# A planned fp32 factorization kernel: first loads entered in the planner's model, X sums in wide operations, two zero matmuls instead of three

## The chip, the core and the metric

The kernel runs on one core of a Trainium2 chip. The core has five engines that work beside each other and wait for one another by semaphores: TensorE (PE: matmuls, with weight loads that overlap them), VectorE (DVE), ScalarE (ACT), GpSimd (POOL) and SyncE (SP, which here only issues transfers). Transfers can be issued by SP, ScalarE and GpSimd and run on the core's 16 DMA engines. The metric is the time on the device in microseconds, the median of several runs.

## The reference

`x` is 1024 x 512, `weight` holds 64 matrices of 512 x 512, `lin_w` is 512 x 512, all in fp32.

```python
out_lin = x @ lin_w.T + lin_b
xv = jnp.einsum('bf,efm->bem', x, weight)
zp = jnp.einsum('bf,efm->bem', jnp.square(x), jnp.square(weight))
interaction = 0.5 * jnp.sum(jnp.square(xv) - zp, axis=1)
return out_lin + interaction
```

The sum of `zp` over `e` needs only the weights' squares summed over `e`, so it is one small matmul at the end. The large work is `xv`, 64 products of 1024 x 512 by 512 x 512, whose squares are summed over `e`.

## The kernel before, in words

**The products.** The weights are laid out beforehand in 16 groups `g`, each four quadrants of 1 MB: `w11`, `w12`, `w21`, `w22` (`w22` in two buffers, `w22a` and `w22b`, used by turns). Within a group the product with x is made by a fast scheme with 7 products in place of 8, applied at two levels. At the outer level, seven operands `X1` to `X7` stand for sums of x's quarters, and each meets one of seven right sides: the four quadrants, `T1`, `T2` (sums of quadrants that DMAs accumulate on the way in) and `w12`, `w21` once more with something added to them. At the inner level each pair of an outer operand and a right side is a "tree" of 7 products. The outer operands come in the order `ORDER = (1, 6, 2, 7, 5, 4, 3)`: the first tree is X1 with `w11`, the second X6 with `T2`, the third X2 with `w21`. There are 16 x 7 = 112 trees.

**One tree** (`tree`). GpSimd makes four inner sums of the right side, `t1` to `t4` (each in a ring of two buffers, so `t1_0` and `t1_1`). TensorE makes the products, each of two matmuls of 128 x 512 ("a pair") into a PSUM tile of two banks. PSUM holds four such tiles: `b1`, `b3` and the ring `b2_0`, `b2_1`. Several products add into one tile after its earlier value was copied away: product 5 starts `b3`, ScalarE copies it to a buffer of the ring `p5`, product 3 is added, and the result is copied to one of the ring `p53`; product 1 starts `b1`, ScalarE copies that to `b2_*`, product 6 is added there, VectorE takes `b2 + p53` out (`oa1<-b2,p53`), product 7 is added, and so on. The next tree's product 5 overwrites `b3`, so it waits for the copy to `p53`. The products of neighbouring trees are interleaved by `PLACE`: product p of tree s has the key 7 s + PLACE[p], and TensorE's order is the order of the keys.

**The squares.** The results of the outer scheme are squared on ScalarE and reduced on VectorE into `acc`. The weights' squares are made by `w_squares`: ScalarE squares half a quadrant into a ring of two buffers `wsq`, VectorE reduces it over `e` into `w2_sum`. For `w22a` of the first group these are the pairs `wsq_0<-w22a` and `wsq_1<-w22a`.

**The beginning.** `xT` comes in eight transfers on SP's queue (into `oa0` to `oa3`) and `lin_wT` in four on ScalarE's (into `ob0`, `ob1`). Meanwhile TensorE runs three matmuls on zeros (lines 323 to 328). Then `lin`, x times `lin_wT`: four k-steps of four pairs into all four PSUM tiles, the last pair put behind the first tree's product 5. VectorE adds the bias and takes the tiles out to `ob2`, `ob3`, `c_0`, `c_1`, and SP writes each of these to DRAM (`lind`). Beside `lin`, the X operands are made: outer sums of 1024 elements a partition (`X7`, `X5`, `X6`, `X3` on VectorE; `X1`, `X2`, `X4` copied by ScalarE), then for each operand four inner sums of 256 elements (lines 392 to 402), all on VectorE.

**The planner.** No engine's order is written out by hand except TensorE's. `Plan.add` records each step with its cost on an engine, what it reads and writes by name, and, for transfers, `land`, the time from the end of the issue to the landing. `Plan.order` first gives each step a latest time, backwards from TensorE's order, and then runs a model of the engines: whenever an engine is free it takes the ready step with the earliest latest time, and may leave a short idle for an urgent one that is about to be ready. What comes out is each engine's order of instructions; on the chip every engine takes its own in that order and waits where a semaphore says so. SP is one engine of the model, with a cost of 4.8 us for a load of 1 MB and 2.4 for a smaller one. The transfers of x and `lin_wT` are issued outside of the plan, ahead of all; the planner only knows when they are taken to have landed (`landing`, lines 309 to 319). In the model, SP is free from the start.

A step marked `both` (the X sums, `x_sum`) gets dearer in the model when GpSimd is busy as it starts, and GpSimd's step with it.

Lines that matter in what follows: 247 and 248 (the X tiles), 309 to 319 (`landing`), 323 to 329 (zeros), 373 to 402 (`x_sum` and its uses), 414 to 416 (`load`), 418 to 424 (`load_more`, the accumulating load that GpSimd issues), 426 to 435 (`outer_sum`). In the profile, L276 is any elementwise sum, L288 a copy on ScalarE, L290 a square, L297 a reduction, L304 a transfer of the plan on SP's queue, L326 the zeros, L340 `lin`, L422 an accumulating load, L481 a tree's matmul, L627 the last matmuls.

Of the kernel before, what the change touches and what calls it, by code (L numbers as in the profile page):

```python
# [11 lines left out]
F32 = mybir.dt.float32  # L12
# [4 lines left out]
P = 128  # L17
G = 2
ORDER = (1, 6, 2, 7, 5, 4, 3)
# [4 lines left out]
PE, DVE, ACT, POOL, SP = "PE", "DVE", "ACT", "POOL", "SP"  # L24
# [148 lines left out]
def kernel(  # L173
# [44 lines left out]
    Q = B // 4  # L218

    sb = ctx.enter_context(tc.tile_pool(name="sb", bufs=1))  # L220
# [9 lines left out]
    buf = {}  # L230

    def make(name, shape, pool=sb):
        buf[name] = pool.tile(shape, F32, tag=name, name=name)
        return name
# [9 lines left out]
        return take  # L244

    half = [P, 2, N]
    for i in range(1, 8):
        make(f"X{i}", [P, 7, Q])
    for q in ("w11", "w12", "w21", "w22a", "w22b", "T1", "T2"):
        make(q, [P, 2, 2, N])  # L250
    for pos in range(4):
# [14 lines left out]
    plan = Plan()  # L266
# [3 lines left out]
    def two_input(engine, o, a, b, sub, size=1024):  # L270

        costs = {DVE: 0.08 + 1.06 * size / 1024, POOL: 0.14 + 2.19 * size / 1024}

        def emit(e):
            f = engines[e].tensor_sub if sub else engines[e].tensor_add
            f(o, a, b)  # L276

        return {engine: costs[engine]}, emit
# [24 lines left out]
    def dma(o, i, reads, writes, cost=2.4, land=1.5, queue=nc.sync):  # L303
        plan.add({SP: cost}, lambda _: queue.dma_start(o, i), reads, writes, land=land)  # L304
# [4 lines left out]
    def landing(name, at):  # L309
        plan.add({SP: 0.0}, None, (), (name,), land=at)  # L310

    for k in range(NK):
        q, r = divmod(k, KH)
        x0, x1, l = f"oa{q}", f"oa{2 + q}", f"ob{q}"
        nc.sync.dma_start(buf[x0][:, r, :], x_src[:, k, ts(0, H)])
        nc.scalar.dma_start(buf[l][:, r, :], lw_src[:, k, :])  # L316
        nc.sync.dma_start(buf[x1][:, r, :], x_src[:, k, ts(1, H)])
        for name in (x0, l, x1):
            landing((name, r), 4.0 + 2.5 * k)
    nc.gpsimd.dma_start(bias, lin_b.partition_broadcast(P))  # L320


    zero = buf["t1_0"]
    nc.vector.memset(zero, 0.0)
    for j in range(3):
        nc.tensor.matmul(  # L326
            buf[("b1", "b3")[j // 2]][:, j % 2, :], zero[:, 0:P], zero, start=True, stop=True
        )
    plan.add({PE: 4.0}, None, (), ("b1", "b3"), key=-2000)

    lin_banks = ["b3", "b1", "b2_0", "b2_1"]
    for k in range(NK):
        q, r = divmod(k, KH)
# [16 lines left out]
    for g, bank in enumerate(lin_banks):  # L350
        o = ("ob2", "ob3", "c_0", "c_1")[g]
        for j in range(G):
            costs, emit = two_input(DVE, buf[o][:, j, :], buf[bank][:, j, :], bias, False, 512)
# [3 lines left out]
    def block4(i):  # L357
        return buf[f"X{i}"][:, 0:4, :].rearrange("p (k q) b -> p k (q b)", k=2)
# [3 lines left out]
    def a_parts(*names):  # L362
        return tuple((a_buf[n], r) for n in names if n in a_buf for r in range(KH)) + tuple(
            n for n in names if n not in a_buf
        )

    def a_ap(n):
        return buf[a_buf[n]] if n in a_buf else block4(int(n[1]))
# [1 line left out]
    for i, n in ((1, "A11"), (2, "A12"), (4, "A22")):  # L370
        act(block4(i), a_ap(n), None, a_parts(n), (f"X{i}",))

    def x_sum(i, o, a, b, kind, reads, size):

        if kind != "-a - b":
            costs, emit = two_input(DVE, o, a, b, kind == "a - b", size)
        else:
            costs = two_input(DVE, o, a, b, True, size)[0]

            def emit(_):  # L380
                nc.vector.scalar_tensor_tensor(o, a, -1.0, b, ALU.mult, ALU.subtract)

        plan.add(costs, emit, reads, (f"X{i}",), both=True)

    for i, a, b, kind in (
        (5, "A22", "A21", "a - b"),
        (6, "X5", "A11", "-a - b"),
        (7, "A11", "A21", "a - b"),
        (3, "X6", "A12", "-a - b"),
    ):  # L390
        x_sum(i, block4(i), a_ap(a), a_ap(b), kind, a_parts(a, b), 1024)
    for i in ORDER:
        x = buf[f"X{i}"]
        a11, a21, a12, a22 = (x[:, s, :] for s in range(4))
        s1, s2, s4 = (x[:, s, :] for s in range(4, 7))
        for o, a, b, kind in (
            (s1, a21, a22, "a + b"),
            (s2, s1, a11, "a - b"),
            (s4, a12, s2, "a - b"),
            (a21, a11, a21, "a - b"),  # L400
        ):
            x_sum(i, o, a, b, kind, (f"X{i}",), 256)
    for n in a_buf.values():
        plan.add({SP: 0.0}, None, (), (n,) + tuple((n, r) for r in range(KH)))
    for n in ("ob0", "ob1", "ob2", "ob3", "c_0", "c_1"):
# [5 lines left out]
    def w(g, q):  # L411
        return q + "ab"[g % 2] if q == "w22" else q

    def load(g, q):
        n = w(g, QUAD[q])
        dma(buf[n], weight[g, q], (), (n,), 4.8)

    def load_more(n, src, reads=()):

        plan.add(  # L420
            {POOL: 1.0},
            lambda _: nc.gpsimd.dma_start(buf[n], src, accum_op=ALU.add),  # L422
            (n,) + reads, (n,), land=8.0,
        )

    def outer_sum(g, which):
        if which < 3:
            n = f"T{which}"
            dma(buf[n], weight[g, 0], (), (n,), 4.8)
            for q in (1, 3)[:which]:  # L430
                load_more(n, weight[g, q])
        elif which == 3:
            load_more("w12", weight[g, 3])
        else:
            load_more("w21", buf["T2"], ("T2",))
# [117 lines left out]
    for g in range(NG):  # L553
        acc_name[g] = acc_ring()
        load(g, 0)
        outer_sum(g, 2)
        for q in (1, 2, 3):
            load(g, q)
        outer_sum(g, 1)
        w_squares(g, "w12")  # L560
        for idx, i in enumerate(ORDER):
            if i == 1:
                w_squares(g, "w11")
            if i == 2:
                w_squares(g, "w21")
            if i == 7:
                outer_sum(g, 3)
            if i == 4:
                outer_sum(g, 4)
            if i == 5:  # L570
                w_squares(g, "w22")
            tree(7 * g + idx, g, i)
        if g + 1 < NG:
            names = tuple((acc_name[g], *k) for k in acc_parts)
            dma(acc_dram[:, :, ts(g, MG)], buf[acc_name[g]], names, names + (("accd", g),))
# [13 lines left out]
    for g in range(NB // G):  # L589
        n, a = lin_all[g], acc_all[g]  # L590
# [3 lines left out]
    for n in xe.values():  # L594
        plan.add(
            {DVE: 1.24},
            lambda _, x=buf[n]: nc.vector.scalar_tensor_tensor(
                x, x, -0.5, x, ALU.mult, ALU.mult
            ),
# [13 lines left out]
    for g in range(NB // G):  # L613
        rows = {0: (2, 3), 1: (4, 5)}[g // 2]
        reads = tuple((last, i, 2 * (g % 2) + c) for i in rows for c in range(2))
# [5 lines left out]
    for g, bank in enumerate(("b3", "b1", "b2_0", "b2_1")):  # L621
        o = acc_all[g]
        h = g // 2
        for j in range(G):
            def emit(_, bank=bank, g=g, h=h, j=j):
                for k in range(NK):
# [9 lines left out]
                     key=last_key - 0.5 if (g, j) == (0, 0) else last_key + 1 + 2 * g + j)  # L636
            costs, emit = two_input(
                DVE, buf[o][:, j, :], buf[bank][:, j, :], buf[lin_all[g]][:, j, :], False, 512
            )
# [37 lines left out]
```

## Time and profile before

| what | us |
|---|---|
| median of 3 runs | 1421.0 |
| lowest and highest | 1420.74, 1421.23 |
| the profiled execution | 1420.72 |
| its span, from the first to the last instruction | 1418.9 |

| engine | busy, us | share of the span |
|---|---|---|
| TensorE, matmuls | 1408.6 | 99% |
| VectorE | 1082.0 | 76% |
| GpSimd | 1014.1 | 71% |
| ScalarE | 681.8 | 48% |

The mean granted clock of TensorE is 0.999 of full speed. From about 2 to 58 us the DMA engines are busy throughout, mostly at 200 to 430 GB/s; over the span they move 142 GB/s.

Matmuls are pipelined in the records: one record of 593 ns begins every 0.43 us. So the start times tell more than the durations do. A line of the timeline gives the start in us from the beginning of the span, the duration, the engine, the line of the code, the operation with its output and input tiles (buffer numbers left out, so `X` is any of X1 to X7), the shape, how many instructions were merged into the line, and, in brackets, the idle time of the engine before it and what ended that.

### The profile page before, as it was taken

To read this page: it belongs to the slowest core of one execution; us is meant where nothing else is said; L and a number is where in the kernel's file an instruction comes from. 1 tells how busy PE (TensorE), PEld (TensorE's weight loads), DVE (VectorE), ACT (ScalarE), POOL (GpSimd) and SP (SyncE) were. 2 spreads that over 40 slices of the span, in tenths; PEclk is the share of its full clock that TensorE was granted. 3 is DMA by queue.
4 is the path that set the end of the run, shared out by engine and by line. 5 is a ranking of instruction groups with operands and counts; after the bars stand their busy time and mean duration, and the time that the engine had idled before them with its cause. 6 is when DMAs were issued, how large, how long until landed. Compare 5 with 4: busy or idle time off the path is not lost.

```text
span 1418.9 us, 10383 instructions
## 1 busy us (share of the span) xinstructions
PE 1408.6 (99%) x3270; PEld 621.9 (44%) x3270; DVE 1082.0 (76%) x957; ACT 681.8 (48%) x692; POOL 1014.1 (71%) x693
## 2 busy tenths in 40 slices
PE   9999999999999999999999999999999999999998
PEld 4444444444444444444444444444444444444443
DVE  4779596876958678596877959687795867869685
ACT  2346363554635446373544636355463644537331
POOL 3587786867769686786958678586777868678660
PEclk9999999999999999999999999999999999999999
DMA  9666372655737275472746637265573727546331
GB/s 327 184 162 167 95 179 74 189 123 148 176 88 162 86 182 148 118 178 73 182 108 168 162 100 182 74 182 122 148 181 90 162 79 191 139 123 144 102 106 60
DMA packets 47286, 200.96 MB, mean 142 GB/s; under 512 B 19008, under 2 KB 20032, under 8 KB 24704
## 3 DMA queue, kind: packets, MB, share of 16 engines
q0 software_dynamic: 11600, 84.15, 31.4%
q1 hardware_dynamic: 35056, 115.09, 22.7%
q10 hardware_dynamic: 576, 1.05, 0.2%
q8 instruction: 27, 0.44, 0.1%
q14 instruction: 27, 0.22, 0.0%
HBM read 177.34 MB, written 6.16 MB: 129 GB/s over the span
## 4 chain that ended last, share of the span: by engine, by line
PE 95%; DMA 2%; DVE 2%; POOL 1%; issue 0%; ACT 0%; ACTq 0%; DVEq 0%; SPq 0%
PE b L481 93%; PE b L627 2%; DMA w<-weight 1%; DVE X L276 1%; DMA ob<-lin_wT 1%; POOL ob L276 0%; POOL c L276 0%; DVE w_sum L297 0%; DVE c L276 0%; DVE ob L276 0%; POOL oa L276 0%; ACT oa L290 0%; ACTq L316 0%; POOL t L276 0%; DVE p L276 0%
## 5 line engine op out<-in xcount | busy, mean ns | idle before, releaser
L481 PE MATMUL b<-t,X 128*128 128x512 f32 x1792 | 808.2, 593 | 4.0 <-DVE oa L276 2.6
L481 PEld LDWEIGHTS b<-t,X 128*128 128x128 f32 x1792 | 340.4, 190 | 434.8 <-issue 429.0
L481 PE MATMUL b<-w,X 128*128 128x512 f32 x768 | 358.1, 592 | 0.0
L276 POOL TENSOR_TENSOR t<-w 128x512 f32<-128x512 f32 x128 | 171.2, 1337 | 147.6 <-PE b L481 91.8
L288 ACT COPY p<-b 128x1024 f32<-128x1024 f32 x160 | 161.1, 1007 | 170.6 <-PE b L481 170.6
L481 PEld LDWEIGHTS b<-w,X 128*128 128x128 f32 x768 | 145.9, 190 | 183.7 <-issue 183.4
L276 POOL TENSOR_TENSOR t<-w,t 128x512 f32<-128x512 f32 x128 | 167.7, 1310 | 57.7 <-PE b L481 57.7
L290 ACT ACTIVATE oa<-oa 128x1024 f32<-128x1024 f32 x128 | 133.7, 1057 | 148.0 <-DVE oa L276 146.1
L297 DVE TENSOR_REDUCE acc<-oa 128x16 f32<-128x1024 f32 x128 | 153.7, 1212 | 39.2 <-ACT oa L290 39.2
L481 PE MATMUL b<-T,X 128*128 128x512 f32 x384 | 180.5, 592 | 0.0
L288 ACT COPY b<-b 128x1024 f32<-128x1024 f32 x112 | 111.8, 999 | 141.0 <-PE b L481 140.5
L297 DVE TENSOR_REDUCE w_sum<-wsq 128x16 f32<-128x1024 f32 x128 | 152.2, 1209 | 9.2 <-ACT wsq L290 9.2
L290 ACT ACTIVATE c<-c 128x1024 f32<-128x1024 f32 x64 | 67.6, 1057 | 160.2 <-DVE c L276 93.7
L276 DVE TENSOR_TENSOR oa<-b,p 128x1024 f32<-128x1024 f32 x96 | 116.9, 1218 | 34.5 <-PE b L481 34.5
L276 POOL TENSOR_TENSOR t<-T 128x512 f32<-128x512 f32 x64 | 85.3, 1333 | 65.7 <-issue 35.4
L481 PEld LDWEIGHTS b<-T,X 128*128 128x128 f32 x384 | 73.1, 190 | 92.4 <-issue 84.9
L276 DVE TENSOR_TENSOR p<-b,p 128x1024 f32<-128x1024 f32 x80 | 97.7, 1221 | 20.8 <-PE b L481 19.1
L276 DVE TENSOR_TENSOR ob<-b,p 128x1024 f32<-128x1024 f32 x48 | 58.6, 1221 | 70.2 <-PE b L481 70.2
L290 ACT ACTIVATE wsq<-w 128x1024 f32<-128x1024 f32 x96 | 98.2, 1057 | 15.1 <-DMA w<-weight 13.3
L276 POOL TENSOR_TENSOR t<-T,t 128x512 f32<-128x512 f32 x64 | 86.4, 1350 | 18.1 <-PE b L481 18.1
L276 DVE TENSOR_TENSOR p<-b,oa 128x1024 f32<-128x1024 f32 x32 | 39.2, 1224 | 65.6 <-PE b L481 65.6
L276 DVE TENSOR_TENSOR oa<-b,oa 128x1024 f32<-128x1024 f32 x64 | 78.3, 1223 | 9.8 <-PE b L481 9.7
(55 smaller groups left out, 1338.7 us busy)
## 6 DMA issues: line engine op xcount, KB each, us to landing
w<-weight SPq DMA_DIRECT2D x48, 1024.0 KB, 4.9
T<-weight POOLq DMA_DIRECT2D x48, 1024.0 KB, 8.2
T<-weight SPq DMA_DIRECT2D x32, 1024.0 KB, 4.8
w<-weight POOLq DMA_DIRECT2D x16, 1024.0 KB, 8.2
w<-T POOLq DMA_DIRECT2D x16, 1024.0 KB, 6.9
w22a<-weight SPq DMA_DIRECT2D x8, 1024.0 KB, 11.1
w22b<-weight SPq DMA_DIRECT2D x8, 1024.0 KB, 11.3
oa<-xT SPq DMA_DIRECT2D x8, 256.0 KB, 6.4
```

Source lines behind the costliest of these rows:

```text
L276: f(o, a, b)
L288: nc.scalar.copy(o, i)
L290: nc.scalar.activation(o, i, func)
L297: lambda _: nc.vector.tensor_reduce(o, i.rearrange("p a (m e) -> p a m e", e=E), axis=AX.X, op=ALU.add),
L481: nc.tensor.matmul(buf[b][:, j, :], buf[f"X{i}"][:, SLOT[p], ts(j, P)], op, start=first, stop=True, skip_group_check=True,)
L627: nc.tensor.matmul(buf[bank][:, j, :], buf[xe[h, k // KH]][:, k % KH, ts((g * G + j) % (NB // 2), P)], w2_sum[:, k, :], start=(k == 0), st ...
```

## The change

- The seven X tiles become slices of one tile `x_all`.
- The inner sums of the first operand in ORDER, X1, stay four operations of 256 elements a partition. Those of X2 to X7 become four operations over all six operands, 6 x 256 elements each; in the plan each reads and writes all six names.
- The zero matmuls go to `b1` only, two instead of three. Their cost in the plan stays 4.0.
- The taken landing times of the first loads are 4.3 + 2.6 k in place of 4.0 + 2.5 k for step k. A name "first loads" that lands at 9.0 is added, and the planned loads of weights through SP (`load`, and the first load into `T1` or `T2` in `outer_sum`) read it, so that in the model none of them is issued before that time. On the chip this is no wait: it only moves what the planner decides.

```diff
     half = [P, 2, N]
+    x_all = sb.tile([P, 7, 7, Q], F32, tag="x_all", name="x_all")
     for i in range(1, 8):
-        make(f"X{i}", [P, 7, Q])
+        buf[f"X{i}"] = x_all[:, i - 1]
...
         for name in (x0, l, x1):
-            landing((name, r), 4.0 + 2.5 * k)
+            landing((name, r), 4.3 + 2.6 * k)
     nc.gpsimd.dma_start(bias, lin_b.partition_broadcast(P))
+    landing("first loads", 9.0)
...
-    for j in range(3):
+    for j in range(2):
         nc.tensor.matmul(
-            buf[("b1", "b3")[j // 2]][:, j % 2, :], zero[:, 0:P], zero, start=True, stop=True
+            buf["b1"][:, j, :], zero[:, 0:P], zero, start=True, stop=True
         )
-    plan.add({PE: 4.0}, None, (), ("b1", "b3"), key=-2000)
+    plan.add({PE: 4.0}, None, (), ("b1",), key=-2000)
...
-        x_sum(i, block4(i), a_ap(a), a_ap(b), kind, a_parts(a, b), 1024)
-    for i in ORDER:
-        x = buf[f"X{i}"]
-        a11, a21, a12, a22 = (x[:, s, :] for s in range(4))
-        s1, s2, s4 = (x[:, s, :] for s in range(4, 7))
+        x_sum((f"X{i}",), block4(i), a_ap(a), a_ap(b), kind, a_parts(a, b), 1024)
+    for lo, hi in ((0, 1), (1, 7)):
+        a11, a21, a12, a22, s1, s2, s4 = (x_all[:, lo:hi, s, :] for s in range(7))
+        names = tuple(f"X{i + 1}" for i in range(lo, hi))
         for o, a, b, kind in (
             (s1, a21, a22, "a + b"),
             (s2, s1, a11, "a - b"),
             (s4, a12, s2, "a - b"),
             (a21, a11, a21, "a - b"),
         ):
-            x_sum(i, o, a, b, kind, (f"X{i}",), 256)
+            x_sum(names, o, a, b, kind, names, Q * (hi - lo))
...
-        dma(buf[n], weight[g, q], (), (n,), 4.8)
+        dma(buf[n], weight[g, q], ("first loads",), (n,), 4.8)
...
-            dma(buf[n], weight[g, 0], (), (n,), 4.8)
+            dma(buf[n], weight[g, 0], ("first loads",), (n,), 4.8)
```

In the built order of instructions the two kernels differ only near the beginning:

| queue | before | after |
|---|---|---|
| SP, behind the five first weight loads | `w22a`, `lind<-ob2`, `lind<-ob3`, `lind<-c_0`, `w22b`, `lind<-c_1`, `w11` of group 1 | `lind<-ob3`, `lind<-ob2`, `w22a`, `lind<-c_1`, `lind<-c_0`, `w11` of group 1, `w22b` |
| VectorE | inner X sums among `w_sum` reductions, bias sums and the first `oa<-b,p` | all X sums ahead of the first bias sum |
| ScalarE | squares of `w11` (two) and `w21` (one) ahead of the first `p53<-b3` | one square of `w11` ahead of it, the others later |
| GpSimd | `t4_0<-w11`, accumulates into T2, `w12`, T1 in a row, `t1_0<-w21` later | accumulate into T2, `t4_0<-w11`, accumulate into `w12`, `t1_0<-w21`, accumulate into T1 |
| TensorE | three zero matmuls | two; all else the same |

More of the change, by code (lines that the diff above doesn't have):

```diff
@@ L371, with x_sum @@
         act(block4(i), a_ap(n), None, a_parts(n), (f"X{i}",))
-    def x_sum(i, o, a, b, kind, reads, size):
+    def x_sum(writes, o, a, b, kind, reads, size):
         if kind != "-a - b":
@@ L381, in emit @@
                 nc.vector.scalar_tensor_tensor(o, a, -1.0, b, ALU.mult, ALU.subtract)
-        plan.add(costs, emit, reads, (f"X{i}",), both=True)
+        plan.add(costs, emit, reads, writes, both=True)
     for i, a, b, kind in (
```

## The prediction

> **What bounds the kernel now.** I read the page's engine row first, then TensorE's waits, then the timeline of the first 60 us engine by engine, then the DMA queues in stretches of 0.5 to 4 us.
>
> ```profile
> PE 1408.6 (99%) x3270; PEld 621.9 (44%) x3270; DVE 1082.0 (76%) x957; ACT 681.8 (48%) x692; POOL 1014.1 (71%) x693
> ```
>
> TensorE is busy 1408.6 of 1418.9 us. Its work is 816 pairs of matmuls (784 of the trees, 16 of `lin`, 16 at the end), four records each; 60 records in 25.91 us (line below) are 1.72 us a pair, and 816 of them 1404 us. So only what interrupts TensorE counts. TensorE's waits are three:
>
> ```profile
> PE b L481 <- DVE oa L276: 2.9, 3, 2.4
> PE b L326 <- DVE t L324: 1.5, 1, 1.5
> PE b L481 <- DVE ob L276: 1.2, 1, 1.2
> ```
>
> Two of the three of `oa` are 0.2 and 0.3 us near the end; all else falls before 50 us. TensorE's timeline there:
>
> ```profile
> 1.46 4.64 PE L326 MATMUL b<-t 128*128 128x512 f32 x6 [1.46 <-DVE t L324]
> 5.93 25.91 PE L340 MATMUL b<-ob,oa 128*128 128x512 f32 x60
> 33.01 1.96 PE L481 MATMUL b<-t,X 128*128 128x512 f32 x4 [1.16 <-DVE ob L276]
> ...
> 45.10 1.88 PE L481 MATMUL b<-T,X 128*128 128x512 f32 x4
> 49.35 3.68 PE L481 MATMUL b<-t,X 128*128 128x512 f32 x4 [2.37 <-DVE oa L276]
> 52.83 1.91 PE L481 MATMUL b<-T,X 128*128 128x512 f32 x4
> 54.58 1.88 PE L481 MATMUL b<-t,X 128*128 128x512 f32 x4
> ```
>
> Columns: start, duration, operation, count, idle before. After the pause of 2.37 us four records take 3.48 us (49.35 to 52.83) where 1.72 is normal. From 54.58 on TensorE is full until 1373. So the pair that starts at 54.58 (product 5 of the third outer operand, bank `b3`) is my yardstick: when the same pair starts in the changed kernel, at full clock, gives the difference in time. VectorE makes both pauses:
>
> ```profile
> 18.04 1.42 DVE L276 TENSOR_TENSOR X<-X 128x256 f32<-128x256 f32 x4
> 28.65 1.22 DVE L297 TENSOR_REDUCE w_sum<-wsq 128x16 f32<-128x1024 f32 x1 [9.19 <-ACT wsq L290]
> ...
> 39.29 8.87 DVE L276 TENSOR_TENSOR X<-X 128x256 f32<-128x256 f32 x8
> 48.08 1.21 DVE L276 TENSOR_TENSOR oa<-b,p 128x1024 f32<-128x1024 f32 x1
> ```
>
> It idles 9.19 us behind a reduction whose load is late, while half its X sums are undone; eight of those then take 8.87 us instead of 8 x 0.34 (2.76 us for eight at 11.28), beside GpSimd, and `oa1<-b2_0,p53_0` starts at 48.08 with TensorE waiting.
>
> **What the Trainium skill says.** "SBUF — State Buffer", Who interferes with whom: a VectorE instruction with two SBUF inputs and a GpSimd one that reads SBUF exclude each other; the 8.87 us agree. "TensorE: Matmul & The Clock Gate", Part 1: an idle array falls to half clock and needs about 3.4 us of work to return; here 3.48 us were slow. It gives about 3.4 us for the idle as well; here a gap of 2.37 was enough and one of 1.16 was not. "DMA: Bandwidth & Descriptors", Queues, rings and completion order: an engine takes packets from the queue rows in turn, within a ring in order. Agreed, 40 to 44 us (packets, MB, share), q1 being SP's queue and q0 GpSimd's accumulating loads:
>
> ```profile
> q0 software_dynamic: 98, 0.67, 80.7%
> q1 hardware_dynamic: 97, 0.33, 22.1%
> ```
>
> 98 against 97 packets. An accumulate alone moves 0.21 MB/us (0.88 MB in 32 to 36, line below), a plain load 0.42 (1.60 MB at 94.5% of 28 to 32).
>
> ```profile
> q0 software_dynamic: 107, 0.88, 105.2%
> ```
>
> **The change, part by part.**
>
> *Zeros.* Two pairs' worth of records go from six to four. At half clock the first four take 1.46 to about 5.07, the last two were 0.43 each at full clock. The first operands landed at about 4.64 (SP's next issue waited until 4.67 for `ob0`), so `lin` starts at 5.07 instead of 5.93: -0.86.
>
> *X sums.* 28 operations of 256 become 4 of 256 and 4 of 1536. No row has 1536; 0.34 for 256 and 1.14 for 1024 (starts 13.96 and 15.10) give 1.04 us per 1024 and 0.07 fixed: 1.67 each. Bounds: 4 x 1.67 alone, or two GpSimd operations of 1.3 in between. VectorE: X7 10.14, X1's four to 12.65, X5, X6, X3 to 16.1, wide ones to 22.8 alone; GpSimd begins at 18.0 (w11's landing), so at worst 25.4. Bank `b3` is complete at 5.07 + 13 x 1.72 = 27.4. So both ends are hidden; X leaves VectorE's queue before `lin` needs it, the 9.19 us idle is harmless, and the 1.2 us wait goes (TensorE gets to product 5 at 30.9, `ob2` is out at 28.9). `oa1<-b2_0,p53_0` then follows its bank at once: the 2.37 us and the 1.76 us of half clock go too.
>
> Without a new wait, product 5 of operand 3 would start at 5.07 + 25 x 1.72 = 48.07 instead of 54.58: -6.5 us.
>
> *The loads.* "first loads" changes SP's order. Before, `w22a` went out at 11.54, directly behind the others, and landed at 32.5. In the built order it now stands behind `lind<-ob3` and `lind<-ob2`, which wait for VectorE: issue at 5.07 + 14 x 1.72 + 1.4 = 30.6 for the first, about 31.9 for `w22a`. Also, on GpSimd, the second accumulate into T2 moves ahead of `t4_0`, and `t1_0<-w21` ahead of T1's accumulate; on ScalarE two squares of w11 and w21 move back. These hide: T2's second accumulate still waits for the first to land (28.1), which w12's load holds back as before.
>
> Who waits for `w22a`: ScalarE's `wsq_0<-w22a`, and behind it in ScalarE's queue the copy `p53_1<-b3`, without which the yardstick pair can't overwrite `b3`. Before, that square ran at 50.84 and the copy at 51.81 with the load long there:
>
> ```profile
> 50.84 1.06 ACT L290 ACTIVATE wsq<-w22a 128x1024 f32<-128x1024 f32 x1 [4.53 <-DVE w_sum L297]
> 51.81 1.00 ACT L288 COPY p<-b 128x1024 f32<-128x1024 f32 x1
> ```
>
> Now TensorE wants `b3` at 48.07, so `w22a` must land by 45.9. When does it? Work for the 16 DMA engines after T1's data end at 29.5: three accumulates (T2, w12, T1, each 1.05 MB) at 0.21 = 15 us; `lind` 2 x 0.52 and `w22a` 1.05 MB at 0.42 = 5 us. The engines are full throughout, 29.5 + 20 = 49.5, and `w22a` is last or nearly: it is behind 1.05 MB of `lind`, whose 4 KB packets took turns with 8 KB accumulates for 12 us before (36.2 to 48.2). The load of the kernel before that stood in the same place is `w22b`, issued at 36.32 behind three such writes:
>
> ```profile
> DMA to landing us min/median/max: 18.5/18.5/18.5
> ```
>
> `w22a`: data end 49.5, landing 0.9 later (0.8 to 1.0 for w12, T1, w22a before) = 50.4, 18.5 after its issue. Square and copy 2.1: TensorE restarts at 52.55 after a pause of 4.5 us, then half clock, +1.76: equivalent start 54.3 against 54.58, -0.3 us. T2's second accumulate, issued at 28.2, has the engines to itself from 29.5 to 34.5 and lands at about 35.9 (lag 1.3 before), and `t1_1` is done at 37.2, before TensorE's 37.75; were it late by up to 4 us, `w22a` would still decide. From there to the end the orders on all engines are the same as before, and no wait of the steady part moves.
>
> **Sum.** Removed 6.5 (by parts 0.86 + 1.28 + 2.53 + 1.76 = 6.4, the waits counted from the end of the pair before by the 1.72 pitch); added 4.48 + 1.76 = 6.2; net -0.3 us. The profiled execution took 1420.72 us (span 1418.9 and 1.8 around it), 0.3 below the median of 1421.0: 1420.4 in that execution, 1420.7 for the median. Own range: landing 49.5 to 52.5 and a second cold window at most, 1419.5 to 1423.4.
>
> **Rivals.**
>
> *Faster: `w22a` is in time.* In the steady part a load lands 4.9 us after issue (section 6); if the order within SP's ring is looser, or writes take a larger share, it lands by 46 to 48. Time 1421.0 - 6.5 = 1414.5 at best, 1418.2 at a landing of 48. For: the packet turns would give a ring with 8 KB packets more bytes. Against: between 36 and 48 us q1 moved only small packets though `w22b` waited.
>
> *Slower: an idle DMA.* Both early accumulates sent their first packet 3.3 to 3.9 us after issue (15.64 to 19.5, 28.21 to 31.5). I read that as waiting for the plain load already under way, since in the steady part it is 1.3 us (606.69 to 608.0). If it is a fixed delay, the engines stand idle from 29.5 to about 31.6, because `w22a` no longer fills that hole. The end moves to 51.6, landing to 52.5 to 53.5 (w22b's lag was 1.9), the pair to 56.4 to 57.4: +1.8 to +2.8, and past +3 if the array stays cold for longer after so long a pause. Time 1423.3. It decides from a first packet later than 30.
>
> *The change does not do what it says:* one operation of 1536 in place of six could cost more than 1.67. Even at 2.8 they end by 27.4, so no time: 1420.7.
>
> **How the numbers follow.** Main reading 0.50 (0.46 within the bound), faster rival 0.27 (0.25 beyond it), slower rival 0.23 (0.11 beyond it). A change under 0.2% (2.8 us) is about what a measurement of this kernel can't tell from none. Faster 0.02 + 0.25 = 0.27, slower 0.02 + 0.11 = 0.13, same 0.60. The range takes in the faster rival whole and the main reading: 1414.4 to 1423.4, leaving out the slower rival's upper half.
>
> **What would show it.** Right: no pause at 31 us, `lin` at 5.1, `oa1` out by 43, a pause of 3 to 5 us before the yardstick pair that ScalarE's copy ends, ScalarE idle on `w22a`'s DMA, and a granted clock near 0.67 behind it. Wrong: `w22a` landing before 46 and TensorE whole from 5 us on (faster), or a DMA share near 0 at 30 us (slower).

## The result and the profile after

The changed kernel takes 1423.76 us (median of 15 runs, 1422.91 to 1424.88), the kernel before 1420.75 in the same set (1416.44 to 1421.23). The ratio is 1.0025, 95% interval 1.0017 to 1.0033: slower by 0.25%, some 3 us, just past the upper end of the range. The profiled execution took 1424.34 us (span 1422.6), 3.6 more than that of before.

TensorE's waits answer the prediction's second fence. Columns: who waited for whom, us in total, times, longest.

```profile
PE b L482 <- ACT p L289: 6.9, 1, 6.9
PE b L328 <- DVE t L326: 1.5, 1, 1.5
PE b L482 <- DVE oa L277: 0.5, 2, 0.3
```

Both pauses that VectorE made (1.2 for `ob`, 2.4 for `oa`) are gone, and one of 6.9 us for a copy of ScalarE has come. TensorE's timeline shows where:

```profile
1.46 3.78 PE L328 MATMUL b<-t 128*128 128x512 f32 x4 [1.46 <-DVE t L326]
5.04 26.45 PE L342 MATMUL b<-ob,oa 128*128 128x512 f32 x60
31.33 1.88 PE L482 MATMUL b<-t,x_all 128*128 128x512 f32 x4
...
46.78 1.88 PE L482 MATMUL b<-T,x_all 128*128 128x512 f32 x4
55.54 7.98 PE L482 MATMUL b<-t,x_all 128*128 128x512 f32 x12 [6.88 <-ACT p L289]
63.35 1.88 PE L482 MATMUL b<-T,x_all 128*128 128x512 f32 x4
```

No pause between 5 and 48 us. The yardstick pair was due at 46.78 + 1.72 = 48.50 and starts at 55.54. The twelve records from there take 63.35 - 55.54 = 7.81 us instead of 12 x 0.429 = 5.15, so 2.66 us go to half clock (TensorE at half its full speed). At full clock the pair would have started at 58.2, against 54.58 before: +3.6 us, which is the whole difference between the two profiled executions. The view by stretches shows the clock there (stretch, its length, then busy us and instructions for PE, PEld, DVE, ACT and POOL; the last three numbers are the granted clock, the DMA share and GB/s):

```profile
55.50:61.00 5.50, 5.46 (x7) 2.38 (x8) 3.82 (x4) 1.86 (x2) 1.27 (x1) 0.53 0.53 220
61.00:70.00 9.00, 9.00 (x22) 3.99 (x21) 3.68 (x3) 2.02 (x2) 6.14 (x4) 1.00 0.00 0
```

ScalarE in the same stretch, and SP's issues:

```profile
43.54 1.01 ACT L289 COPY oa<-b 128x1024 f32<-128x1024 f32 x1 [0.38 <-PE b L482]
53.53 1.06 ACT L291 ACTIVATE wsq<-w22a 128x1024 f32<-128x1024 f32 x1 [8.98 <-DMA w22a<-weight]
54.49 0.99 ACT L289 COPY p<-b 128x1024 f32<-128x1024 f32 x1
```

```profile
31.12 1.06 SPq L305 DMA_DIRECT2D lind<-ob  x2
32.23 0.65 SPq L305 DMA_DIRECT2D w22a<-weight  x1
36.29 1.90 SPq L305 DMA_DIRECT2D lind<-c  x2
```

ScalarE stands idle for 8.98 us behind a square of `w22a`, and the copy that TensorE needs is the next in its queue. `w22a`'s load went out at 32.23 and landed at about 53.45, 21.2 us later; before, it went out at 11.54 and landed at 32.5. VectorE, the bound of the stretch before, is ahead of its work:

```profile
16.73 9.98 DVE L277 TENSOR_TENSOR x_all<-x_all 128x1536 f32<-128x1536 f32 x4
28.09 1.29 DVE L277 TENSOR_TENSOR ob<-b,t 128x512 f32<-128x512 f32 x2 [1.38 <-PE b L342]
...
41.83 1.23 DVE L277 TENSOR_TENSOR oa<-b,p 128x1024 f32<-128x1024 f32 x1 [0.21 <-PE b L482]
```

The wide operations took 2.5 us each, with GpSimd at work beside them, and VectorE still waited 1.38 us for TensorE's `b3`.

### The profile page after: what moved, and what is told of

It reads as the page before. It is cut to its first block, busy times and chain, and to the rows that moved or that the text cites. A ratio compares the mean times of both kernels' runs of the same rounds, so it can differ in the third digit from the quotient of the medians.

```text
span 1422.6 us, 10355 instructions
## 1 busy us (share of the span) xinstructions
PE 1408.9 (99%) x3268; PEld 622.1 (44%) x3268; DVE 1078.5 (76%) x937; ACT 681.2 (48%) x692; POOL 1014.6 (71%) x693
## 4 chain that ended last, share of the span: by engine, by line
PE 96%; DMA 1%; POOL 1%; ACT 0%; DVE 0%; issue 0%; SPq 0%; DVEq 0%; ACTq 0%
PE b L482 92%; PE b L628 2%; PE b L342 2%; DMA w22a<-weight 1%; POOL ob L277 0%; POOL c L277 0%; PE b L328 0%; POOL oa L277 0%; ACT oa L291 0%; DVE ob L277 0%; DVE p L277 0%; POOL t L277 0%; ACT wsq L291 0%; SPq L305 0%; ACT b L289 0%
## 5 line engine op out<-in xcount | busy, mean ns | idle before, releaser
L482 PE MATMUL b<-t,x_all 128*128 128x512 f32 x1792 | 809.0, 594 | 7.3 <-ACT p L289 6.9
L482 PEld LDWEIGHTS b<-t,x_all 128*128 128x128 f32 x1792 | 341.0, 191 | 439.0 <-issue 428.1
L482 PE MATMUL b<-w,x_all 128*128 128x512 f32 x768 | 358.1, 592 | 0.0
L482 PEld LDWEIGHTS b<-w,x_all 128*128 128x128 f32 x768 | 145.9, 190 | 183.7 <-issue 183.4
L482 PE MATMUL b<-T,x_all 128*128 128x512 f32 x384 | 180.4, 592 | 0.0
L482 PEld LDWEIGHTS b<-T,x_all 128*128 128x128 f32 x384 | 73.0, 190 | 91.8 <-issue 84.9
```

The lines of the kernel that those rows point to most:

```text
L482: nc.tensor.matmul(buf[b][:, j, :], buf[f"X{i}"][:, SLOT[p], ts(j, P)], op, start=first, stop=True, skip_group_check=True,)
```

## The experiments

All were timed in five rounds beside the kernel before, whose median in these sets was 1419.6 to 1420.1; a ratio below is to it. For nearly every profiled execution the time is the (full-clock) start of the yardstick pair plus 1366.1 to 1366.5 us (before 1420.72 - 54.58, after 1424.34 - 58.2), so that one start is compared throughout. A move in a diff, written in words here, is a move in the planner's finished list (`ops`), from which the instructions are put out; it changes the order on one engine and nothing else.

**1. `w22a_first`: is it the load's place on SP?**

```diff
+    move(load of w22a, behind load of T1)
```

> The changed kernel with one DMA issue moved: the first load of w22a is issued on SP directly behind T1's load, as before, and no longer behind the two lin_dram stores; every other engine keeps its order. Theory (the place of that load is the whole loss): w22a lands long before 45 us, the 6.88 us wait of the yardstick pair for ACT's copy goes, its half clock too, and the pair starts at 48.5, or up to 2.5 us later if T2's accumulating loads, which again share the DMA engines with w22a, let product 1 on T2 wait as in the kernel before. Time 1414.6 to 1417, about 4 to 6 us under the kernel before. Rival A (the wide sums, two and a half times as dear beside GpSimd as alone, or the missing zeros are what costs): no more than the 1 us of half clock comes back, 1423 to 1424. Rival B (DMA traffic as such is late, whatever the order): the wait moves to T2 at 38 us and keeps over half of its length, 1419 to 1421.

1416.1 us (1415.83 to 1416.25), ratio 0.9972 [0.9962, 0.9983]. The pause is gone and the pair starts at 50.01, after 0.51 us for T2's `t`. One transfer's place is 7.7 us; with it back, the rest of the change is a gain of about 4 us. The start is later than 48.5 for a second reason: half clock at the beginning lasted to 7.59, in the profile of the changed kernel to 6.11, which cost the first records of `lin` 0.74 us more.

**2. `copy_first`: is it the copy behind the square?** The load stays late.

```diff
+    later = {wsq_0<-w22a: p53_2, its reduction: ob3, wsq_1<-w22a: b2_0, its reduction: ob2}
+    each key is moved behind its value
```

> The changed kernel with w22a's load where the change put it (behind the two lin_dram stores), but with the two squares of w22a moved on ACT behind the copies p53_1, b2_1, oa2 and p53_2, and the two reductions on VectorE behind ob3 and ob2. Theory (the late load costs only because ACT's copy p53_1 stands behind the square): w22a still lands at about 53.5, TensorE does not pause at the yardstick pair, which starts at 48.5, and the time is 1424.3 less 9.7 = 1414.6 (1414 to 1416). Rival (late transfers hurt in any case, because T1, w11 or w22b are late behind w22a, or because VectorE or GpSimd needs it): a pause of over 3 us appears within the next 30 us, 1418 or more.

1414.64 us (1414.56 to 1414.95), ratio 0.9964 [0.9951, 0.9976], the fastest of all kernels here. TensorE's timeline:

```profile
46.76 1.88 PE L482 MATMUL b<-T,x_all 128*128 128x512 f32 x4
48.47 5.31 PE L482 MATMUL b<-t,x_all 128*128 128x512 f32 x12
53.62 1.88 PE L482 MATMUL b<-T,x_all 128*128 128x512 f32 x4
```

The load was issued at 31.71 and landed 21.0 us later, at 52.7, nearly as late as in the changed kernel, and nobody was held up: the twelve records take 5.15 us. So the late data alone cost nothing. The loss was in the instructions queued behind the one that waits, here ScalarE's copy (the two reductions on VectorE were moved along). It was 1423.76 - 1414.64 = 9.1 us.

**3. `no_model_part`: the change without the scheduler's part**

```diff
-    landing("first loads", 9.0)
-            landing((name, r), 4.3 + 2.6 * k)
+            landing((name, r), 4.0 + 2.5 * k)
...
-        dma(buf[n], weight[g, q], ("first loads",), (n,), 4.8)
+        dma(buf[n], weight[g, q], (), (n,), 4.8)
```

> The changed kernel without the scheduler's part: loads cost the model nothing at the start again (no first-loads entry, landing times 4.0 + 2.5 k), while the four wide operations and the two zero pairs stay. The planner then issues w22a behind T1, puts the copy p53_1 ahead of both squares of w22a and spreads the wide operations between ob2, ob3 and the reductions. Theory: the part in the model alone is the loss, so this is faster than before: the first and second pauses shrink, the yardstick pair starts at 49 to 51, time 1415 to 1417.5. Rival (wide sums or zeros lose the time): 1422 or more.

1416.79 us (1416.53 to 1417.07), ratio 0.9976 [0.9968, 0.9985]. The planner puts `w22a` behind T1's load again. A pause of 1.61 us for `ob` is left (one wide operation now stands behind a late reduction on VectorE), and the pair starts at 50.30.

**4. `model_part_alone`: the scheduler's part on the kernel before.** The diff is the reverse of the last one, put on the kernel before.

> The kernel before with the scheduler's part of the change alone (first-loads entry and landing times); narrow sums and three zero pairs stay. The planner puts w22a's load behind the two lin_dram stores here too, all narrow sums ahead of ob2 on VectorE, and on ACT p53_1 ahead of the squares of w22a, with b2_1's copy behind both squares. Theory: w22a lands at 53 to 54, the wait falls on product 6 of outer operand X6, which needs b2_1 and would be due at about 52.9; the copy is done at 56.5, so a pause of about 3.5 us plus 2 us at half clock, against the 5 to 6 us that the earlier pauses cost before. If the 13 narrow sums that VectorE now does in its idle 9 us end by 29, 1419.5 to 1422; if they keep VectorE beyond 32, 1 to 4 us more. Rival (the model part is harmless without the wide sums): 1417 or less, without a pause of TensorE between 50 and 60.

1415.77 us (1414.63 to 1416.11), ratio 0.9971 [0.9962, 0.9980]: the rival won. The part that loses in the changed kernel gains 4 us on its own, with `w22a`'s load behind the same two stores. The tile's view gives the time from issue to landing; first the changed kernel, then this one:

```profile
DMA to landing us min/median/max: 21.2/21.2/21.2
```

```profile
DMA to landing us min/median/max: 9.9/9.9/9.9
```

Issued at 33.6, it lands at 43.5. GpSimd's timeline says why; again the changed kernel first:

```profile
28.28 0.88 POOL L423 DMA_DIRECT2D T<-weight  x1 [3.18 <-DMA T<-weight]
28.89 1.57 POOL L277 TENSOR_TENSOR t<-w,t 128x512 f32<-128x512 f32 x1
30.14 1.15 POOL L423 DMA_DIRECT2D w<-weight  x1
```

```profile
28.47 0.88 POOL L423 DMA_DIRECT2D T<-weight  x1 [1.24 <-DMA T<-weight]
29.09 1.58 POOL L276 TENSOR_TENSOR t<-w,t 128x512 f32<-128x512 f32 x1
34.64 1.28 POOL L276 TENSOR_TENSOR t<-w 128x512 f32<-128x512 f32 x1 [3.98 <-PE b L482]
35.86 0.86 POOL L423 DMA_DIRECT2D w<-weight  x1
```

The planner put `t1_0<-w21` ahead of the accumulating load into `w12` here. The first instruction waits for TensorE, so that load went out at 35.86 and not at 30.14. DMA queues from 36 to 41 us (packets, MB, share of 16 engines), the changed kernel, then this one:

```profile
q0 software_dynamic: 99, 0.81, 77.7%
q1 hardware_dynamic: 99, 0.41, 21.5%
```

```profile
q1 hardware_dynamic: 367, 1.84, 103.6%
```

With no accumulate beside it SP's ring moves 1.84 MB in 5 us and not 0.41: both stores and most of `w22a`. A new theory follows: the load was late for two reasons together, its place behind the stores on SP and the accumulates that GpSimd sends in the same stretch. Experiments 5 and 6 test it from both sides.

**5. `acc_later`: the changed kernel with GpSimd's accumulates later**

```diff
+    move(accumulate into T1, behind t2_1<-T2)
+    move(accumulate into w12, behind t1_1<-T2)
```

> The changed kernel with two DMA issues moved on GpSimd: w12's accumulating load behind t1 on T2, T1's behind t2 on T2 (in the changed kernel both go out directly behind T2's second one); SP, ACT and VectorE keep their order, so w22a's load stays behind the two lin_dram stores and its first square ahead of p53_1. Theory (new, from the trace of model_part_alone, where w22a's load in the same place on SP landed 9.9 us after its issue and not 21: the DMA engines were then free of accumulating loads from 35.8 to 41): the two stores and w22a run from 35.5 at 0.4 MB in a us, w22a is over at about 40.9 and lands at 42 to 43.5, there is no pause at the yardstick pair (48.5 to 49.9), and the time is 1414.4 to 1416. Rival (the place on SP alone decides, as the prediction had it, with GpSimd's order of no account): w22a lands after 50, 1421 or more. Rival (w12's or T1's later sum is late for GpSimd, and so for the third outer operand's trees): a pause of over 2 us between 60 and 75, 1417 to 1420.

1417.65 us (1416.52 to 1419.16), ratio 0.9984 [0.9978, 0.9991]. `w22a` lands 9.4 us after its issue, at 42.0, TensorE does not pause, and the pair starts at 48.89. The theory holds against the first rival. The second rival was right in the time, and a little over in the pause (1.55 and 0.37 us, for over 2): GpSimd now waits for the later sums (7.29 us for `w12`), and VectorE behind it holds TensorE at 69 us:

```profile
66.06 1.88 PE L482 MATMUL b<-w,x_all 128*128 128x512 f32 x4
69.49 1.98 PE L482 MATMUL b<-w,x_all 128*128 128x512 f32 x4 [1.55 <-DVE p L277]
```

**6. `model_acc_early`: the accumulates early in `model_part_alone`**

```diff
+    move(accumulate into T1, behind accumulate into w12)
+    move(t1_0<-w21, between the two)
```

> model_part_alone with GpSimd's accumulating loads where the changed kernel has them: w12's directly behind T2's second one, T1's directly behind t1 on w21. Nothing else moves. Theory: w22a (behind the two stores on SP) then lands at 53 to 55 instead of 43.5; p53_1 stands ahead of its squares on ACT here, so the yardstick pair keeps its 49.8, and the pause falls on product 6 of X6, due at 53.3, whose b2_1 copy comes behind both squares at about 56.3: 2.5 to 4 us of pause and about 2 at half clock, time 1419 to 1422.5. Rival (GpSimd's order is of no account, something else made w22a early): 1415.8 as model_part_alone.

1420.68 us (1417.73 to 1422.84), ratio 0.9999 [0.9991, 1.0007], 4.9 us over `model_part_alone`. `w22a` lands 18.8 us after its issue, at 51.9, and ScalarE waits 4.76 us for it. The pause of 2.00 us is where it was expected, at the product that needs `b2_1`. The profiled execution is the fastest of the 13: no half clock followed, and the load came a little earlier and the pause was a little shorter than expected.

**7. `w22a_between`: half of the stores ahead of the load**

```diff
+    move(store from ob2, behind load of w22a)
```

> The changed kernel with w22a's load on SP between the two lin_dram stores (ob3, w22a, ob2): 0.52 MB of small packets ahead of it in SP's ring in place of 1.05. Theory (the ring moves 0.085 MB in a us while GpSimd's accumulating loads run, and w22a gets 0.14 to 0.16 in their company): the store is through at about 42, w22a has 0.85 to 0.95 MB by 48 and the rest by 48.6, lands at 49.5 to 51, the wait is 3 to 4.5 us: 1419.5 to 1421.5. Rival (what is ahead in SP's ring does not matter, the accumulating loads alone decide when it ends): over 52.5 and 1423 or more. Rival (the place behind any store is what matters only through the issue time): w22a lands before 46 and 1415.5 or less.

1421.24 us (1419.14 to 1422.49), ratio 1.0008 [1.0000, 1.0016]; beside it on the same chip the changed kernel took 1423.64. The load lands at 51.2, the wait is 4.85. Time as expected, landing and wait a little past the expected ends. Half the bytes ahead in the ring are worth only about 1.5 us of landing against 52.7 in the repeat below; the accumulates moved out of its way (experiment 5) are worth 10.7. Of what makes the load late, the accumulates beside it weigh more than the stores ahead of it.

**8. `c_later`: do the two later stores prolong the landing?**

```diff
+    move(stores from c_1 and c_0, behind load of w22b)
```

> The changed kernel with the two lin_dram stores from c_0 and c_1 issued behind w22b's load and no longer between w22a's load and w11's; everything else keeps its order. Theory for the landing (w22a's bulk is over at about 50.7, and it lands only at 53.45 because the c stores' small packets stand on the same DMA engines beside and ahead of its end): w22a lands at 51.3 to 52, the wait of the yardstick pair is 4.8 to 5.5 instead of 6.88, time 1422 to 1423. Rival (the lag of 2.7 us between the bulk and the landing belongs to the load itself, or to the two stores ahead of it): landing at 53 to 53.7 and 1423.6 to 1424.4. Either way the kernel stays slower than before.

1422.8 us (1421.65 to 1423.65), ratio 1.0021 [1.0013, 1.0029]; landing about 52.3 and wait 5.71, between the two expectations, the time within the first. It was repeated beside the changed kernel on one chip.

> The changed kernel once more, beside the next two on the same chip. It tells how far w22a's landing, the wait behind it and the stretch at half clock vary from one execution to the next: if the lag of 2.7 us from the last of w22a's bulk (about 50.7) to its landing (53.45) belongs to this order, it is 2.3 to 3.1 again and the time within 1423.3 to 1424.3; if it is chance, 1 to 2 and the profiled time at 1422 to 1423.

> c_later once more, now beside the changed kernel on the same chip. If the two stores from c_0 and c_1 prolong w22a's lag, the median is 0.7 to 1.9 us under after_again's with intervals that do not overlap; if the lag is chance, within 0.5 us of it.

`after_again` 1423.64 (1423.19 to 1424.11), landing 52.7, wait 6.26; `c_later_again` 1422.93 (1421.9 to 1423.91), landing 52.0, wait 5.22. Twice 0.7 to 1.0 us in the direction of the theory, but the ranges overlap, and so do the intervals of the ratios (1.0027 [1.0017, 1.0036] and 1.0020 [1.0013, 1.0027]). If the stores do it, they are worth 1 us of time at most. Not settled.

**9. `w22a_first_narrow`: are the wide operations worth anything?** Experiment 1 with 24 operations of 256 in place of the four wide ones.

```diff
+            plan.ops[-1].emit = lambda e: [op(o[:, i], a[:, i], b[:, i]) for i in range(hi - lo)]
```

> w22a_first with each wide operation written as six operations of 256 elements in the same place (24 in place of 4); nothing else moves. Theory: the wide form is worth only what VectorE's cover doesn't hide. The four wide ones took 9.98 us from 17.08 and VectorE then idled 1.77 us before ob2. 24 narrow ones take 8.2 us at 0.34 each where GpSimd is idle, and up to 1.1 each beside it: end between 26 and 36. If by 28.8, the time is w22a_first's 1416.1; if at 31 to 33, ob2 is late by 1 to 3 us, and product 5 of the first outer operand waits for it: 1417 to 1419. Rival (wide sums are what brings the gain): beyond 36, VectorE the bound of the whole stretch, 1420 or more.

1416.26 us (1415.99 to 1416.88) against 1416.1. The 24 take 11.34 us, the four wide ones 9.98, and `ob` is in time with both:

```profile
16.68 11.34 DVE L405 TENSOR_TENSOR x_all<-x_all 128x256 f32<-128x256 f32 x24
28.24 1.29 DVE L277 TENSOR_TENSOR ob<-b,t 128x512 f32<-128x512 f32 x2 [0.22 <-PE b L342]
```

In this order the wide form brings no measurable time.

**10. `sums_early`: is it VectorE's order?** The kernel before, one order changed.

```diff
+    first = first reduction of a weight's squares on VectorE
+    ops = ops[:first] + (X sums behind it) + (everything else behind it)
```

> The kernel before with only VectorE's order changed: all narrow sums of x (28 of 256 elements) go ahead of the two reductions of w12's squares, for which VectorE idled 9.19 us; the load model, the zeros, the other engines keep their order. Theory (what the change gains over before is the order of VectorE's work, not the wide form: w22a_first with narrow sums took 1416.26 against 1416.1): the sums end before 28.6, the first pause (1.26, VectorE's ob2) shrinks to about 0.7, since both reductions still stand ahead of ob2, and the second one (2.31, oa1 behind five late narrow sums) goes with its half clock: 1416 to 1418. Rival (the wide form or the model part is needed): 1419 or more.

1416.09 us (1415.64 to 1416.18), ratio 0.9971 [0.9960, 0.9983]. Both pauses of the kernel before are gone, and the pair starts at 49.92. That the second one goes is the order's doing: `oa1<-b2_0,p53_0` starts at 43.33 and not at 48.08. The first one this execution can't tell: half clock at the beginning lasted to 7.19 and not to 5.11, so TensorE came to product 5 at 32.72, where it had come at 31.85 before and waited. Most of what the change gains is this order (3.6 us here, 4.0 in experiment 1), which needs neither the wide form nor the planner's new entries.

**11. The zeros**

```diff
-    for j in range(3):
-            buf[("b1", "b3")[j // 2]][:, j % 2, :], zero[:, 0:P], zero, ...
+    for j in range(2):
+            buf["b1"][:, j, :], zero[:, 0:P], zero, ...
```

`zeros_alone` is this on the kernel before, `copy_first_zero3` the reverse on `copy_first`.

> The kernel before with two zero pairs of two records each in place of three; the order is that of before. Theory: TensorE's lin products start at 5.04 to 5.1 instead of 5.93, some of them at half clock, and what is left of the 0.86 us is taken up by the first pause, which VectorE's ob2 ends at 32.9 whatever TensorE did: 1420 to 1421.2, no change. Rival (the zeros' 0.86 us comes through to the end): 1419.2 to 1420.0 where before has its upper cluster at 1421.0. Rival that costs: half clock at the start for over 2 us more, first tree product after 33.4, 1421.5 or more.

> copy_first with the third zero pair put back. Theory (the zero edit is worth its records less the half clock that it leaves in the lin products): the lin products start at 5.93 at full clock instead of 4.82, the first tree product at 31.6 instead of 30.68, nothing downstream takes that up, so the time is 0.9 us over copy_first: 1415.5 (1415.2 to 1415.8). Rival (the start isn't on the path, since a later wait sets the pace): 1414.6. Rival (two pairs leave the clock at half for as long again, as in w22a_first, where the first tree product came at 32.06): 1414.2 or less.

`zeros_alone`: 1419.47 (1419.09 to 1421.11), ratio 0.9999 [0.9991, 1.0007], no change. In the two profiled executions there was no gain that the first pause could take up: half clock lasted to 6.94 and not to 5.11, which cost as much as the two records that are left out, and TensorE came to the pause at 31.90, before at 31.85. `copy_first_zero3`: 1415.32 (1415.17 to 1415.83) against 1414.64, so the pair is worth 0.7 us where nothing takes it up. Half clock at the start ended between 4.6 and 7.6 us in these profiles, so a difference of this size between single executions is not safe.

**12. `first_loads_4`: a mend in the planner's own terms**

```diff
-    landing("first loads", 9.0)
+    landing("first loads", 4.0)
```

> The changed kernel with the landing of the first loads in the scheduler's model at 4.0 instead of 9.0; the planner then issues w22a's load directly behind T1's, ahead of the lin_dram stores, and puts one reduction of w12 ahead of ob2 and the fourth wide operation behind ob3. Theory: w22a lands at about 33, no pause at the yardstick pair; the reduction waits for w12's square to about 29.8 and ob2 comes at 31 to 32, so the first pause returns with 0.3 to 1.5 us: 1415 to 1417. Rival (the 9.0 has a worth of its own elsewhere): 1418 or more.

1415.87 us (1415.77 to 1415.96), ratio 0.9968 [0.9956, 0.9981]. The planner issues `w22a` behind T1's load again, and the pair starts at 49.67. One number changed keeps the gain and loses the wait.

## Why the prediction was wrong

*Zeros, -0.86.* About right alone where nothing takes it up (0.7 in experiment 11), but it doesn't count: the later wait for `w22a` ends at the same time whatever TensorE did before. The sum also let `lin` run at full clock from its start at 5.07; it started at 5.04 and ran at half clock until 6.11. That is why the pair was due at 48.50 and not at 48.07.

*X sums, the pauses gone, pair due at 48.07: -6.5.* Right in size. It started at 48.47 in `copy_first`: -6.1. The wide operations took 9.98 us and not 6.7, past the prediction's worst end (26.7 against 25.4), still inside their cover. (The 1.04 us are for 1000 elements, not 1024; the 1.67 that follow are right.) The stated cause was too narrow: the order does it, not the form (9 and 10).

*The new wait.* Place, waiter and chain were right word for word: load behind the stores, square, copy, `b3`. Experiments 1 and 2 each take one link out, and each brings 7.7 to 9.1 us.

*"Data end 49.5, landing 0.9 later = 50.4": this step failed.* The load landed at 53.45, because its data ended at 53.16. First, the bulk was 1.2 us late. Counting SP's bytes from 36 us on, 2.10 MB (two stores and `w22a`) are reached at about 50.7. T2's accumulate started slowly (0.07 MB from 29 to 30 us and 0.11 in the next, then 0.2 in each) and kept the engines until 35.7 and not 34.5. Second, there was a tail of 2.5 us. `w22a` is 128 packets of 8 KB, the stores are packets of 4 KB. 123 of the 128 had started by 50.50. The other five started one after another at 51.05, 51.93, 52.24, 52.54 and 52.85, while the rest of SP's ring was already at the later stores. From 50.51 to 53.10, all but five packets are small:

```profile
DMA packets 258, 0.95 MB, mean 369 GB/s; under 512 B 30, under 2 KB 30, under 8 KB 253
```

The prediction let all engines end together. One DMA engine that was behind the others would look like this, but the trace doesn't name the engine, and why it was behind stays open. From the end of the last packet to the landing it took 0.3 us, less than the 0.9 allowed for. In the repeat the last packet ended at 52.14 and in `model_acc_early` at 51.49, with landings 0.6 and 0.4 later: the tail is what differs from run to run. The prediction had seen its size in `w22b`, the load in the same place behind stores, as a lag of 1.9, and gave it to the rival only. So TensorE started again at 55.54 instead of 52.55: +3.0.

*"Then half clock, +1.76": mis-sized.* It measured 2.66: +0.9. The prediction took over the loss of another pause. But in these traces the clock changes only at the ends of stretches of 3.41 us (last section): before, it fell at 49.48, just behind the restart at 49.35, and rose one stretch later; here it had fallen at 53.90, TensorE came back at 55.54, inside the stretch, and it rose only after one more, at 60.73. Sum: -0.3 + 3.0 + 0.9 = +3.6, the difference of the profiled executions.

*T2 on time, nothing later moved.* Right: no other pause, T2 landed at 36.1 for 35.9.

*The slower rival* had nearly the price, 1423.3, and named the longer cold stretch. Its mechanism was not what happened: T2's first packet came at 29.89, 1.6 us after the issue and as T1's data ended, so the engines did not stand idle to 31.6. The prediction was at fault in the width: with the same chain, a lag of 1.9 and a longer cold stretch belonged in the main reading's own range, which ended at 1423.4.

*"The engines are full throughout" was right, but the prediction drew too little from it.* With the engines full, the load's end depends on what GpSimd sends beside it. The prediction costed GpSimd's reordering by its own waits ("these hide") and never asked what the accumulates' place does to `w22a`. Experiments 4 to 6 show that it is as much a cause as the place on SP: either one alone leaves the yardstick pair without a pause (50.01 in experiment 1, 49.84 in 4, 48.89 in 5).

## What to carry to other kernels

A late transfer is priced by what stands behind its first consumer in that engine's queue, so list that queue before costing the transfer: here the same late landing cost 9 us or nothing. When the DMA engines are full, ask of each transfer what runs beside it, and don't let its last packets end with the average: take a range from the load that stood in the most similar place. Give the half clock behind a pause a range: here it was 0.1 to 2.7 us. Try a gain credited to a new form of operation with the old form in the new order.

## What the runs showed of the hardware

What a pause of TensorE costs in clock depends on where it falls, not only on its length. Half clock and its end are read from the traces' clock records; loss is what the records behind the pause took beyond 0.429 us each:

| kernel | pause, us | TensorE restarts | half clock | loss, us |
|---|---|---|---|---|
| `model_acc_early` | 2.00 | 54.98 | none | 0.1 |
| `zeros_alone` | 2.31 | 49.43 | none | 0.2 |
| before | 2.37 | 49.35 | 49.48 to 52.89 | 1.8 |
| `w22a_between` | 4.85 | 53.31 | 53.52 to 56.93 | 1.8 |
| `c_later_again` | 5.22 | 54.11 | 50.97 to 57.80 | 1.9 |
| `c_later` | 5.71 | 54.40 | 52.42 to 59.24 | 2.5 |
| `after_again` | 6.26 | 54.80 | 52.68 to 59.51 | 2.4 |
| after | 6.88 | 55.54 | 53.90 to 60.73 | 2.7 |

The loss is half of the time that TensorE worked at half clock: in the changed kernel (60.73 - 55.54) / 2 = 2.6. The half clock lasted 3.41 or 6.83 us, once or twice the same stretch, and from the first rise of the clock to its fall it is 13 or 14 such stretches (before 44.37 us, after 47.79). The Trainium skill, "TensorE: Matmul & The Clock Gate", Part 1, says that a free-running window of about 3.4 us decides; these times agree. Cut into such stretches (columns as above), first the kernel before, then the changed one:

```profile
46.07:49.48 3.41, 1.04 (x4) 0.21 (x3) 3.41 (x6) 0.24 (x1) 1.14 (x1) 1.00 0.98 247
49.48:52.89 3.41, 3.41 (x5) 1.35 (x6) 3.41 (x5) 2.05 (x3) 0.00 (x0) 0.50 1.02 422
52.89:56.30 3.41, 3.41 (x9) 1.50 (x8) 2.71 (x3) 1.86 (x2) 1.28 (x1) 1.00 1.03 426
```

```profile
47.07:50.49 3.42, 1.59 (x4) 0.38 (x2) 0.00 (x0) 0.00 (x0) 1.22 (x1) 1.00 0.99 369
50.49:53.90 3.41, 0.00 (x0) 0.00 (x0) 0.00 (x0) 0.37 (x1) 0.00 (x0) 1.00 1.03 383
53.90:57.31 3.41, 1.77 (x2) 0.84 (x3) 2.69 (x3) 3.41 (x4) 0.00 (x0) 0.50 1.00 422
57.31:60.73 3.42, 3.42 (x5) 1.35 (x4) 2.01 (x2) 0.05 (x1) 1.27 (x1) 0.50 0.32 132
60.73:64.14 3.41, 3.41 (x9) 1.52 (x8) 0.53 (x1) 1.01 (x1) 1.80 (x2) 1.00 0.00 0
```

TensorE's busy time in one stretch goes with the clock of the next. After 1.04 us of work or none the clock fell, after 1.59 it stayed full. At half clock, 1.77 us of work were not enough to raise it, a full stretch was. The other traces of the table agree: the highest share after which it fell is 1.33 us (`c_later_again`). The same part of the skill lets the clock fall after an idle window; here one with 1.33 us of work in it was enough, and the measurement decides. So the pause of 2.37 us, which lay within one stretch, cost as much as the one of 4.85, and the pause of 2.31, cut in two by the end of a stretch, cost none.

This would also fit the times of the kernel before, most of which lie near 1421.0 and near 1419.4, about one such loss apart: its traced execution paid at the second pause and took 1420.72, that of `zeros_alone` did not pay and took 1419.22. Its other executions were not traced, so this is a guess. A few of them took only 1416.4 to 1416.8 us (5 of 34 in the last set), nearly as little as the kernels of experiments 1, 10 and 12; why stays open.

Beside GpSimd, either engine may pay. In the changed kernel GpSimd's first two sums took 4.42 us (later ones, alone, 1.27 each) and VectorE's four wide operations 9.98. In `model_part_alone` the same two took 7.72 and VectorE's 17 narrow sums 5.79, their price alone (0.34 each).
